# Moments of two tiles at once, and biases carried as the last row of difference weights

## The chip, the cores and the metric

The kernel runs on one core of a Trainium2 chip. The metric is device time in microseconds (us), the median of several executions. A profile is one execution, recorded instruction by instruction.

## The reference

The input u has 8 sequences of 512 steps and 128 features, in float32. Four layers follow, each added to its own input, and each fed with a layer norm without gain:

```
x = x + ssm(layernorm(x))          # diagonal state-space recurrence over time
x = x + linear(layernorm(x))       # one of 8 weight matrices (128 x 128), picked by logits, with its bias
x = x + delta_rule(layernorm(x))   # 16 heads of 8 features, a state of 8 x 8 per head, step by step
x = x + moe(layernorm(x))          # 8 experts, the best 2 of a softmax router
```

The parts that matter here:

```
def _layernorm(x, axis=-1, eps=1e-05):
    m = jnp.mean(x, axis=axis, keepdims=True)
    v = jnp.var(x, axis=axis, keepdims=True)
    return (x - m) / jnp.sqrt(v + eps)
...
def _l2_bounded(W, bound=1.0):               # in the first layer, for W_in and W_out
    sigma = jnp.linalg.svd(W, compute_uv=False)[0]
    return W / jnp.maximum(sigma / bound, 1.0)
...
out = jnp.einsum('btd,de->bte', x, W[idx]) + b[idx]          # second layer
...
logits = xf @ w_router                                        # fourth layer
h = jnp.einsum('te,ieh->tih', xf, w1) + b1                    # 8 experts, 128 -> 512
h = jax.nn.gelu(h)
out = jnp.einsum('tih,ihe->tie', h, w2) + b2
```

A row that comes out of the layer norm sums to zero over its 128 features. So for such a row, x W is the sum over the first 127 features of x_d (W_d - W_127), where W_127 is the last row of W.

## The kernel before, in words

**Tiles and groups.** A tile is 16 time steps of all 8 sequences: 128 rows of 128 features, one row on each of the 128 partitions. There are 32 tiles, taken in 8 groups of 4. Up to three layers of different groups are in work at once. The experts work on "chunks" of `GROUPS`: first one group of 4 tiles, then three times 8 tiles, then 4 tiles.

**First layers.** `input_statistics` takes the layer norm's numbers of the input of all groups early: `moments` runs bn_stats and bn_aggr for each tile on VectorE, and `factors` makes from mean and variance the factor and the shift on POOL (GpSimd). The u of later groups is loaded for that into the five buffers named `w1b`. `load_x` loads u once more for the layers themselves, into two buffers named `x`. `scanned` is the state-space layer up to its scan, `ssm_out` its output, scaled by `gain`, and `linear` the second layer, with the picked weights `wsel` and the picked bias `bsel` that POOL gathers from DRAM at the start.

**The gain.** It needs the largest singular value of W_in and of W_out. `spectral` squares W^T W `SQUARINGS` times on TensorE, for the two matrices in turn, with a trace every third step that keeps the numbers in range. The two are on VectorE and ScalarE: `copied` and `scaled` differ. At the end two sums (`total`) give the value.

**Delta rule.** `delta_in` makes keys, queries, values and beta of a group with TensorE, ScalarE and POOL, writes keys and queries to a DRAM buffer (`scratch`), and prepares small matrices (`tmat`). `delta_rule` is the recurrence. For each tile SP loads `kq` (two buffers of 2,048 columns, 1 MB each) from `scratch` and `vals` into `so`; then VectorE runs four blocks of six instructions each, one after the other, since each block needs the state that the block before leaves. There are 128 blocks. POOL and TensorE turn `so` into the tile's output x3.

**Experts.** `route` takes the layer norm of x3 into tiles `xne`, the router's logits, the two best experts and their weights. `experts` counts rows for each expert, scatters the rows by indirect DMAs on POOL's queue into a DRAM table (`places`) in which every block of 128 rows belongs to one expert, and goes through the blocks: SP loads up to four blocks of rows (`xb`) and for each block the expert's first weights (`w1b`, by a register that holds the expert's row in `w1b_dram`), TensorE makes `ph`, ScalarE the gelu into `hid`, TensorE the second product. The results go to DRAM (`results`), POOL gathers them back by row (`back`), and they are weighted and added. A chunk of 4 tiles makes 15 blocks and one of 8 makes 23: 99 in all. The weights in `w1b_dram` have 516 columns: 512 of w1, and 4 with the expert's bias, as a column for each quarter of the 512. ScalarE's gelu takes that column as its bias, one call for each quarter.

**The order.** The code does not run in the order in which it is written. Each call goes through a recorder (line 317) into a `Plan`, which knows each operation's engine, an estimated cost, and which operations it must follow. `Plan.best` makes `DRAFTS` drafts of an order by list scheduling, with due times (`nc.key`) that it changes at random from a fixed seed, and keeps the draft that ends first by its own costs. That order is then fixed: each engine and the queue of SP run their instructions one after another, and an instruction that waits holds all behind it on its engine. Almost all instructions so bear line 317 in the profile, and are told apart by the names of their buffers.

Of the kernel before, what the change touches and what calls it, by code (L numbers as in the profile page):

```python
# [17 lines left out]
P = 128  # L18
# [6 lines left out]
NHB = 4  # L25
SQUARINGS = 24
FIRST = 9
# [313 lines left out]
def _cost(engine, name, n, kw):  # L341

    if engine == "tensor":
        return 0.2 if name == "transpose" else 0.22 + 0.0019 * max(_size(kw["rhs"])[1] - 96, 0)
    if engine == "vector":
        if name == "tensor_tensor_scan":
            return 0.1 + 0.0026 * n
        return 0.19 + 0.00103 * n + (0.2 if n == 9 * 32 else 0.0)
    if engine == "scalar":
        columns = sum(isinstance(kw.get(k), bass.AP) for k in ("bias", "scale"))  # L350
        return 0.18 + 0.00085 * n + (0.0, 0.0001 * n, 0.13)[columns]
    return 0.22 + 0.0015 * n if n < 64 else 0.4 + 0.0017 * n

# [3 lines left out]
BEHIND = 8.0  # L357
DRAFTS = 60
JITTER = 15
# [7 lines left out]
def seq_kernel(  # L367
# [72 lines left out]
    def ctile(shape, name, dtype=F32):  # L440
        return const.tile(shape, dtype, tag=name, name=name)
# [18 lines left out]

    WIDE = {"both": 2 * N, "xne": P, "w1b": NHB * P + NHB, "drive": N + B, "z": N + B, "kq": NR * QN, "prod": B * BL * BL}

# [4 lines left out]
    def stile(shape, tag, dtype=F32, bufs=2):  # L467
        return turn(
            "small_" + tag, bufs, lambda name: pipe.tile(shape, dtype, tag=name, name=name)
        )[tuple(slice(0, m) for m in shape)]  # L470
# [35 lines left out]

    R_BP, R_AL, R_DB, R_G, R_B, R_QKVB, R_B1 = 0, 3, 4, 5, 6, 7, 11
    n_rows = R_B1 + NE * NHB
    rows = ptile([n_rows, P], "hid", 3)
    nc.scalar.dma_start(rows[R_BP : R_BP + 3], bp.rearrange("(c p) -> c p", p=P))  # L510
    for r, v in ((R_AL, alpha_log), (R_DB, delta_bias), (R_G, ln_g), (R_B, ln_b)):
        nc.scalar.dma_start(rows[r : r + 1], v.rearrange("(c p) -> c p", p=P))
    nc.scalar.dma_start(rows[R_QKVB : R_QKVB + 4], b_qkvb.rearrange("(c p) -> c p", p=P))
    nc.scalar.dma_start(rows[R_B1:], b1.rearrange("e (c p) -> (e c) p", p=P))
    lg_col = ctile([P, 1], "lg_col")
# [10 lines left out]
    wr = ctile([P, NE], "wr")  # L526
    nc.sync.dma_start(wr, w_router)

    b2_sb = ctile([NT * NE, NT, D], "b2_sb")
# [122 lines left out]
    def col(r):  # L652
        return cols[:, r : r + 1]


    FW = NHB * P + NHB
    w1b_dram = dram.tile([NE * P, FW], F32, tag="w1b_dram", name="w1b_dram")
    nc.key = 0.0
    nc.sync.dma_start(w1b_dram[:, 0 : NHB * P], w1.rearrange("e d f -> (e d) f"))
    nc.sync.dma_start(  # L660
        w1b_dram[:, NHB * P :].rearrange("(e p) c -> p e c", p=P),
        cols[:, R_B1:].rearrange("p (e c) -> p e c", c=NHB),
    )

# [39 lines left out]
    w_row = ctile([P, 1], "w_row", U32)  # L704
    nc.vector.tensor_copy(w_row, pk[:, 4:5])
    b_row = ctile([P, 1], "b_row", U32)
    nc.vector.tensor_copy(b_row, topi[:, 0:1])
    wsel = ctile([P, D], "wsel")
    bsel = ctile([P, D], "bsel")
    for dst, src, row in (  # L710
        (wsel, ffn_W.rearrange("e d f -> (e d) f"), w_row),
        (bsel, ffn_b, b_row),
    ):
        nc.gpsimd.indirect_dma_start(
            out=dst[:, :],
            out_offset=None,
            in_=src,
            in_offset=bass.IndirectOffsetOnAxis(ap=row[:, :1], axis=0),
        )


    def moments(src, part, bufs=2):

        n = src.shape[1]
        st = stile([P, NT, 6], "st" + part)
        mv = stile([P, NT, 2], "mv" + part, F32, bufs)[:, 0:n]
        for i in range(n):
            nc.vector.bn_stats(st[:, i, :], src[:, i, :])
            nc.vector.bn_aggr(mv[:, i, :], st[:, i, :])
        return mv  # L730

    def factors(mv, part, norms=1, bufs=2):

        n = mv.shape[1]
        rstd = stile([P, norms, NT], "rstd" + part, F32, bufs)[:, :, 0:n]
        nc.gpsimd.tensor_scalar_add(rstd[:, 0], mv[:, :, 1], LN_EPS)
        if norms == 2:

            nc.gpsimd.tensor_scalar(rstd[:, 1], mv[:, :, 1], 1.0 + LN_EPS, LN_EPS * LN_EPS, ALU.mult, ALU.add)
        nc.gpsimd.tensor_tensor(rstd, rstd, mhalf[:, 0:norms, 0:n], ALU.pow)  # L740
        shift = stile([P, norms, NT], "shift" + part, F32, bufs)[:, :, 0:n]
        nc.gpsimd.tensor_mul(shift, mv[:, :, 0].unsqueeze(1).to_broadcast([P, norms, n]), rstd)
        nc.gpsimd.tensor_scalar_mul(shift, shift, -1.0)
        return rstd, shift
# [3 lines left out]

    def normalised(src, rstd, shift, xn, norm=0):
        for i in range(src.shape[1]):  # L750
            nc.scalar.activation(
                xn[i], src[:, i, :], AF.Identity, bias=shift[:, norm, i : i + 1], scale=rstd[:, norm, i : i + 1]
            )
        return xn

    def tiles_of(v):
        return [v[:, i, :] for i in range(v.shape[1])]
# [22 lines left out]
    def over_tiles(v, n):  # L780
        return v.unsqueeze(1).to_broadcast([P, n, D])
# [93 lines left out]
    def linear(x1):  # L875

        n = x1.shape[1]
        rstd, shift = statistics(x1, "a")
        xT = ptile([P, n * P], "f", FIRST)
        nc.scalar.copy(xT, transposed(normalised(x1, rstd, shift, tiles_of(ptile([P, n, D], "f", FIRST)))))  # L880
        x1b = ptile([P, n, D], "f", FIRST)
        nc.gpsimd.tensor_add(x1b, x1, over_tiles(bsel, n))
        x2 = ptile([P, n, D], "x2", 2)
        nc.vector.tensor_add(x2, tokens_out(xT, wsel), x1b)
        return x2
# [178 lines left out]
    def route(g, x3, group):  # L1064
# [3 lines left out]
        rstd, shift = statistics(x3, "e")  # L1068
        x3n = normalised(x3, rstd, shift, [ptile([P, D], "xne", MAXT) for _ in range(NT)])
        x3T = ptile([P, N], "x3T")  # L1070
# [94 lines left out]
    def experts(group):  # L1165
# [144 lines left out]
        def hidden_of(j):  # L1310
# [16 lines left out]
            for c in range(NHB):  # L1327
# [3 lines left out]
                )  # L1331
            for c in range(NHB):
                cs = slice(c * P, (c + 1) * P)
                nc.scalar.activation(
                    hid[:, cs], ph[:, cs], AF.Gelu_apprx_tanh, bias=w1b[:, NHB * P + c : NHB * P + c + 1]
                )
            return hid
# [66 lines left out]
    sp = ctile([P, 24], "sp")  # L1404
    smax, rmax, rtr, sums, lam, sig = (sp[:, i : i + 2] for i in (0, 2, 6, 8, 12, 14))
    nc.vector.tensor_reduce(smax, w_both, AX.X, ALU.max, apply_absolute_value=True)
# [13 lines left out]
    def spectral(i, copied, scaled):  # L1420

        c = slice(i, i + 1)
        junk = ptile([P, P], ("x3T", "fin")[i])

        def power():
            return ptile([P, P], ("xbT", "xne")[i], (2, MAXT)[i])

        def total(x, y, column):

            sums_ = part[:, 2 * column + i : 2 * column + i + 1]  # L1430
            if x is y:
                nc.scalar.activation(junk, x, AF.Square, accum_out=sums_)
            else:
                nc.vector.tensor_mul(junk, x, y)
                nc.vector.tensor_reduce(sums_, junk, AX.X, ALU.add)
            at = ph_tile()[:, 0:1]
            nc.tensor.matmul(
                at, lhsT=ones, rhs=part[:, 2 * column + i : 2 * column + i + 1], start=True, stop=True
            )
            return at  # L1440

        cur, a0 = power(), ptile([P, P], f"back{i}")
        scaled(cur, w_both[:, i, :], rmax[:, c])
        factor = None
        for step in range(SQUARINGS + 1):
            bank = po_tile()
            nc.tensor.matmul(bank[:, 0:P], lhsT=cur, rhs=cur, start=True, stop=True)
            if step % 3 == 0 and step < SQUARINGS:


                trace = total(cur, cur, 0)
                nc.vector.tensor_scalar_max(rtr[:, c], trace, 1e-18)
                nc.vector.reciprocal(rtr[:, c], rtr[:, c])
                nc.vector.tensor_mul(rtr[:, c], rtr[:, c], rtr[:, c])
            cur = a0 if step == 0 else power()
            if step % 3 == 1:
                scaled(cur, bank[:, 0:P], rtr[:, c])
            else:
                copied(cur, bank[:, 0:P])
            yield  # L1460
        nc.vector.tensor_copy(sums[:, c], total(cur, a0, 0))
        nc.vector.tensor_scalar_max(rtr[:, c], total(cur, ident, 1), TINY)
        nc.vector.reciprocal(rtr[:, c], rtr[:, c])
        yield

# [3 lines left out]
    for _ in zip(  # L1469
        spectral(0, nc.vector.tensor_copy, vector_scaled), spectral(1, nc.scalar.copy, nc.scalar.mul)  # L1470
    ):
        pass
    nc.vector.tensor_mul(lam, sums, rtr)
    nc.gpsimd.tensor_tensor(sig, lam, half, ALU.pow)
# [23 lines left out]
    for g in range(1, NG):  # L1498
# [4 lines left out]
        input_statistics(g, x)  # L1503

    x2s = {g: first_layers(g) for g in range(2)}
    for g in range(NG):
# [70 lines left out]
```

## Time and profile before

| | |
|---|---|
| median of 14 runs | 772.32 us (768.63 to 777.38) |
| the profiled execution | 774.93 us, of it 773.2 us span from the first to the last instruction |
| granted TensorE clock, mean | 0.811 |
| TensorE matmul busy | 524.3 us (68%), 2,948 instructions |
| VectorE busy | 526.7 us (68%), 1,468 instructions |
| ScalarE busy | 469.1 us (61%), 1,062 instructions |
| POOL busy | 549.0 us (71%), 681 instructions |
| gelu, x396 | 114.0 us on ScalarE, 380 ns each |
| DMA | 105.94 MB, 137 GB/s in the mean |

How to read it: the busy times are means over stages with different limits, so a stage is read from the busy times in its own stretch of time. In a timeline a line gives the start, the duration, the engine, the line of the kernel, the operation, `out<-in` by the names of the buffers, the shapes, the count, and in brackets how long the engine had been idle and what ended that. `SPq` is SP's queue, which issues DMAs: the duration there is that of the issue, not of the transfer.

### The profile page before, as it was taken

The page shows a single profiled execution, that of the slowest core. Times are in us where ns is not written, and L with a number is a line of the kernel's source. Part 1 is how long each engine was busy: PE and PEld are TensorE (multiplying, and loading weights), DVE is VectorE, ACT ScalarE, POOL GpSimd, SP SyncE. Part 2 cuts the span into 40 slices and gives each one's busy share as a digit, 9 for nine tenths or more (in the row PEclk, how much of TensorE's full clock was granted, in tenths as well). Part 3 has the DMA queues.
Part 4 walks back from the last instruction along what each step waited for, and adds up shares of the span by engine and source line. Part 5 has one row for each costly group of instructions (what it writes and reads, how often), then busy time and mean ns, then how long its engine had stood idle before and what let it go on. Part 6 is the DMA issues. An engine that isn't in the chain of part 4 may idle for free. (4 is left out here: it accounts for less than half of the span.)

```text
span 773.2 us, 11166 instructions
## 1 busy us (share of the span) xinstructions
PE 524.3 (68%) x2948; PEld 408.1 (53%) x2948; DVE 526.7 (68%) x1468; ACT 469.1 (61%) x1062; POOL 549.0 (71%) x681
## 2 busy tenths in 40 slices
PE   5884664874861886894687888397893677568190
PEld 4662224453541464682465766385783576568190
DVE  5764189989997999999599999679896563000103
ACT  3855756655854899986668878248562346446060
POOL 6658575776688996998699997975887476732603
PEclk9755576786895889996698999879997699879686
DMA  3725242532435643654554864748686476656332
GB/s 105 211 73 170 64 94 60 137 76 58 115 97 150 165 119 83 178 150 136 141 136 122 206 174 123 195 127 201 184 205 170 134 189 174 162 149 183 88 97 78
DMA packets 97717, 105.94 MB, mean 137 GB/s; under 512 B 9100, under 2 KB 72535, under 8 KB 97655
## 3 DMA queue, kind: packets, MB, share of 16 engines
q1 hardware_dynamic: 92992, 96.66, 47.7%
q0 software_dynamic: 4160, 8.53, 4.0%
q8 instruction: 25, 0.41, 0.2%
q14 instruction: 38, 0.30, 0.1%
q10 hardware_dynamic: 502, 0.03, 0.0%
HBM read 81.26 MB, written 23.94 MB: 136 GB/s over the span
## 5 line engine op out<-in xcount | busy, mean ns | idle before, releaser
L317 ACT ACTIVATE hid<-ph,w1b 128x128 f32<-128x128 f32 x396 | 114.0, 380 | 79.9 <-remote 28.2
L317 PE MATMUL ph<-xbT,w1b 128*128 128x128 f32 x792 | 121.1, 297 | 29.6 <-ACT xbT L317 21.9
L317 PEld LDWEIGHTS ph<-xbT,w1b 128*128 128x128 f32 x792 | 110.2, 210 | 44.2 <-ACT xbT L317 24.3
L317 POOL DMA_INDIRECT back<-results,small_dest x64 | 63.0, 984 | 57.3 <-DVE fin L317 26.6
L317 DVE TENSOR_TENSOR so<-kq,st 128x512 f32<-128x512 f32 x128 | 87.5, 684 | 15.9 <-PE in L317 7.4
L317 DVE TENSOR_REDUCE st<-so 128x32 f32<-128x288 f32 x128 | 84.1, 657 | 3.5
L1297 PE MATMUL po<-w_sb,hid 128*128 x536 | 80.6, 288 | 8.1 <-ACT hid L317 4.9
L1297 PEld LDWEIGHTS po<-w_sb,hid 128*128 128x128 f32 x536 | 72.8, 202 | 16.2 <-issue 8.6
L1235 POOL DMA_INDIRECT places<-xne,small_dest x64 | 64.5, 1007 | 21.7 <-issue 14.1
L286 ACT ACT_TABLE_LOAD x52 | 66.7, 1283 | 6.3 <-DMA hid<-in_L_ffn_b_dram 5.4
L317 PE MATMUL po<-wo,so 128*128 128x128 f32 x256 | 44.9, 330 | 33.4 <-DVE so L317 15.3
L317 DVE TENSOR_REDUCE st<-st 128x64 f32<-128x320 f32 x128 | 63.6, 497 | 4.0
L317 PEld LDWEIGHTS po<-wo,so 128*128 128x128 f32 x256 | 41.2, 239 | 43.6 <-DVE so L317 16.5
L317 PE MATMUL in<-b,head_ones 128*128 128x512 f32 x80 | 52.1, 744 | 8.4 <-ACT kn L317 2.2
L317 DVE TENSOR_TENSOR st<-kq,st 128x256 f32<-128x256 f32 x128 | 54.7, 428 | 4.2
L317 DVE TENSOR_REDUCE st<-prod 128x32 f32<-128x128 f32 x128 | 37.6, 294 | 24.9 <-ACT upd L317 15.4
L317 PE MATMUL in<-f,wT 128*128 128x512 f32 x64 | 43.3, 769 | 15.2 <-ACT qkp L317 5.4
L1297 PE MATMUL in<-w_sb,hid 128*128 x256 | 38.0, 290 | 20.1 <-ACT hid L317 17.2
L317 POOL TENSOR_TENSOR qkp<-qkp,upd 128x512 f32<-128x512 f32 x32 | 38.9, 1216 | 17.5 <-ACT upd L317 17.5
L317 POOL TENSOR_TENSOR so<-so 128x512 f32<-128x512 f32 x24 | 30.5, 1272 | 24.7 <-DVE so L317 19.4
L317 PE MATMUL in<-b,wqkvb 128*128 128x512 f32 x64 | 41.4, 746 | 9.4 <-ACT beta L317 4.3
L317 DVE SCALAR_TENSOR_TENSOR fin<-back,small_weight,fin 128x128 f32<-128x128 f32 x16 | 5.2, 350 | 62.2 <-DMA back<-results,small_dest 57.9
(292 smaller groups left out, 1311.9 us busy)
## 6 DMA issues: line engine op xcount, KB each, us to landing
kq<-scratch SPq DMA_DIRECT2D x64, 512.0 KB
w1b<-w1b_dram SPq DMA_DIRECT2D x99, 258.0 KB
xb<-places SPq DMA_DIRECT2D x21, 256.0 KB
results<-yb SPq DMA_DIRECT2D x21, 256.0 KB
places<-yb SPq DMA_DIRECT2D x2, 1472.0 KB
x<-in_L_attn_u_dram SPq DMA_DIRECT2D x32, 64.0 KB
w1b_dram<-in_L_ffn_w_dram SPq DMA_DIRECT2D x1, 2048.0 KB
scratch<-qn SPq DMA_DIRECT2D x8, 256.0 KB
```

The costliest lines, as they stand in the source:

```text
L286: self.hw.scalar.preload_act_table_set(switch)
L317: return method(*(on(x) for x in args), **{k: on(x) for k, x in kw.items()})
L1235: rows_out = hw.gpsimd.indirect_dma_start(out=table[0 : nblk * P, :], out_offset=bass.IndirectOffsetOnAxis(ap=at, axis=0), in_=src, in_off ...
L1297: return hw.tensor.matmul(out_.on(nc.banks), lhsT=src, rhs=w2_f[:, bass.ds(at + c * P, P)], start=(c == 0), stop=(c == NHB - 1),)
```

## The change

- `moments`: one bn_stats over two tiles, read alternately, so that its two halves (count, mean and sum of squared deviations of the even and the odd elements) are the two tiles' moments. The bn_aggr is gone; `factors` divides by 128.
- Biases: the layer norm's rows keep their first 127 features, and a 1 stands in the place of the last. The weights become the difference to their last row, and the bias takes the last row's place: for `wsel`, for the router (without a bias), and for w1. So `linear` needs no addition of the bias.
- The first expert weights, once: the two halves of w1 (4 experts each) are loaded into the two `kq` buffers, the last rows of all experts, spread over all partitions, into `so` and two `xb` buffers; VectorE subtracts (`fold_weights`), and SP writes 127 partitions of each half to `w1b_dram`. Row 127 of each expert comes from b1 directly. `w1b_dram` has 512 columns.
- Gelu: one call for a block of 512 columns.
- `spectral`: 23 squarings, fewer small steps in the trace, and the closing sums made from one more product and one squaring call.
- The planner makes 150 drafts, and knows a cost for memset.

```diff
-SQUARINGS = 24
+SQUARINGS = 23
...
+    if name == "memset":
+        return 0.15 + 0.0008 * n
...
-DRAFTS = 60
+DRAFTS = 150
...
+    wr_last = ctile([P, NE], "wr_last")
+    nc.sync.dma_start(wr_last, w_router[D - 1].partition_broadcast(P))
+    nc.gpsimd.tensor_sub(wr, wr, wr_last)
...
-    FW = NHB * P + NHB
+    FW = NHB * P
     w1b_dram = dram.tile([NE * P, FW], F32, tag="w1b_dram", name="w1b_dram")
     nc.key = 0.0
-    nc.sync.dma_start(w1b_dram[:, 0 : NHB * P], w1.rearrange("e d f -> (e d) f"))
-    nc.sync.dma_start(
-        w1b_dram[:, NHB * P :].rearrange("(e p) c -> p e c", p=P),
-        cols[:, R_B1:].rearrange("p (e c) -> p e c", c=NHB),
-    )
+    nc.sync.dma_start(w1b_dram.rearrange("(e p) f -> e p f", p=P)[:, D - 1, :], b1)
+    nc.key = -100.0
+    w_parts = [ptile([P, 4, FW], "kq", 2) for _ in range(2)]
+    for h, part in enumerate(w_parts):
+        nc.sync.dma_start(part, w1[4 * h : 4 * h + 4].rearrange("e d f -> d e f"))
+    lasts = [so[:, e * FW : (e + 1) * FW] for e in range(6)] + [ptile([P, FW], "xb", 3) for _ in range(2)]
+    for e0, n, dst in ((0, 6, so[:, 0 : 6 * FW]), (6, 1, lasts[6]), (7, 1, lasts[7])):
+        row = w1[e0, D - 1]
+        nc.sync.dma_start(
+            dst.rearrange("p (e f) -> p e f", f=FW), bass.AP(row.tensor, row.offset, [[0, P], [D * FW, n], [1, FW]])
+        )
+
+    def fold_weights():
+        for h, part in enumerate(w_parts):
+            nc.key = -75.0
+            for i in range(4):
+                nc.vector.tensor_sub(part[:, i], part[:, i], lasts[4 * h + i])
+            to = w1b_dram[4 * h * P : 4 * (h + 1) * P].rearrange("(e p) f -> p e f", p=P)
+            nc.sync.dma_start(to[0 : P - 1], part[0 : P - 1])
...
         (wsel, ffn_W.rearrange("e d f -> (e d) f"), w_row),
+        (wlast, ffn_W.rearrange("e d f -> (e d) f"), last_row),
         (bsel, ffn_b, b_row),
...
+    nc.vector.tensor_sub(wsel, wsel, wlast)
+    nc.vector.scalar_tensor_tensor(wsel, bsel, ident[:, P - 1 : P], wsel, ALU.mult, ALU.add)
...
-        for i in range(n):
-            nc.vector.bn_stats(st[:, i, :], src[:, i, :])
-            nc.vector.bn_aggr(mv[:, i, :], st[:, i, :])
+        for i in range(0, n, 2):
+            nc.vector.bn_stats(
+                mv[:, i : i + 2].rearrange("p i s -> p (i s)"), src[:, i : i + 2, :].rearrange("p i d -> p d i")
+            )
...
-        nc.scalar.copy(xT, transposed(normalised(x1, rstd, shift, tiles_of(ptile([P, n, D], "f", FIRST)))))
-        x1b = ptile([P, n, D], "f", FIRST)
-        nc.gpsimd.tensor_add(x1b, x1, over_tiles(bsel, n))
+        xn = ptile([P, n, D], "f", FIRST)
+        nc.gpsimd.memset(xn[:, :, D - 1 : D], 1.0)
+        nc.scalar.copy(xT, transposed(normalised(x1, rstd, shift, tiles_of(xn), 0, D - 1)))
         x2 = ptile([P, n, D], "x2", 2)
-        nc.vector.tensor_add(x2, tokens_out(xT, wsel), x1b)
+        nc.vector.tensor_add(x2, tokens_out(xT, wsel), x1)
...
-            for c in range(NHB):
-                cs = slice(c * P, (c + 1) * P)
-                nc.scalar.activation(
-                    hid[:, cs], ph[:, cs], AF.Gelu_apprx_tanh, bias=w1b[:, NHB * P + c : NHB * P + c + 1]
-                )
+            nc.scalar.activation(hid, ph, AF.Gelu_apprx_tanh)
...
-            if step % 3 == 0 and step < SQUARINGS:
-                trace = total(cur, cur, 0)
-                nc.vector.tensor_scalar_max(rtr[:, c], trace, 1e-18)
+            if step % 3 == 0:
+                nc.vector.tensor_scalar_max(rtr[:, c], squares(cur), 1e-18)
                 nc.vector.reciprocal(rtr[:, c], rtr[:, c])
-                nc.vector.tensor_mul(rtr[:, c], rtr[:, c], rtr[:, c])
...
-        nc.vector.tensor_copy(sums[:, c], total(cur, a0, 0))
-        nc.vector.tensor_scalar_max(rtr[:, c], total(cur, ident, 1), TINY)
+        bank = po_tile()[:, 0:P]
+        nc.tensor.matmul(bank, lhsT=a0, rhs=cur, start=True, stop=True)
+        nc.vector.tensor_scalar_max(rtr[:, c], squares(cur), TINY)
         nc.vector.reciprocal(rtr[:, c], rtr[:, c])
+        nc.vector.tensor_mul(a0, cur, bank)
+        nc.vector.tensor_reduce(part[:, 2 + i : 3 + i], a0, AX.X, ALU.add)
+        nc.vector.tensor_mul(lam[:, c], rtr[:, c], summed(1))
...
+    for x in [ptile([P, D], "xne", MAXT) for _ in range(MAXT)]:
+        nc.gpsimd.memset(x[:, D - 1 : D], 1.0)
...
+    fold_weights()
     x2s = {g: first_layers(g) for g in range(2)}
```

## The prediction

> **What bounds the kernel now.** I read the page first (VectorE's busy tenths in 40 slices), then the busy times by stage.
>
> ```profile
> span 773.2 us, 11166 instructions
> DVE  5764189989997999999599999679896563000103
> ```
>
> ```profile
> 0.00:99.00 99.00, 67.62 (x215) 43.57 (x216) 48.79 (x220) 61.25 (x142) 63.15 (x98) 0.69 0.45 127
> 99.00:640.00 541.00, 380.08 (x2144) 291.97 (x2144) 462.95 (x1187) 355.90 (x758) 428.75 (x525) 0.84 0.54 140
> 640.00:773.20 133.20, 76.65 (x593) 72.61 (x591) 14.96 (x62) 52.00 (x163) 57.06 (x60) 0.80 0.49 131
> ```
>
> After the span the columns are PE, PEld, DVE, ACT, POOL, then clock, DMA share and GB/s. There are three stages with three limits. Up to about 99 us no engine is full: a chain of short steps. From 99 to 640 the VectorE is busy 463 of 541 us: the recurrence, 128 blocks of six instructions. After 640 the VectorE is nearly done and TensorE, ScalarE and gathers alternate. So an edit is worth something in the first stage only if it moves the recurrence's start, and in the second only if it shortens VectorE. The timelines of VectorE, ScalarE and the SP queue show what sets that start.
>
> ```profile
> 70.22 0.69 DVE L317 TENSOR_TENSOR x<-in,f 128x512 f32<-128x512 f32 x1 [5.81 <-ACT f L317]
> ...
> 92.60 0.69 DVE L317 TENSOR_TENSOR drive<-f,in 128x512 f32<-128x512 f32 x1 [19.97 <-POOL f L317]
> ...
> 104.96 0.67 DVE L317 TENSOR_TENSOR so<-kq,st 128x512 f32<-128x512 f32 x1
> ```
>
> ```profile
> 82.60 1.64 ACT L317 ACTIVATE f<-x,small_shifti,small_rstdi 128x128 f32<-128x128 f32 x4
> ...
> 88.68 0.67 ACT L317 ACTIVATE qn<-in,nbq 128x512 f32<-128x512 f32 x1
> ```
>
> ```profile
> 28.12 10.05 SPq L317 DMA_DIRECT2D w_sb<-in_L_ffn_w_dram  x2
> ...
> 59.81 2.71 SPq L317 DMA_DIRECT2D x<-in_L_attn_u_dram  x4
> 64.40 3.83 SPq L317 DMA_DIRECT2D places<-yb  x2
> 89.37 0.36 SPq L317 DMA_DIRECT2D scratch<-qn  x1
> 90.28 0.36 SPq L317 DMA_DIRECT2D scratch<-kn  x1
> 92.00 2.51 SPq L317 DMA_DIRECT2D kq<-scratch  x4
> ```
>
> The first product with kq, at 104.96, is the recurrence's start. It needs the scratch writes and kq loads of SP's queue, and these need ScalarE, which at 82.60 reads the x loaded from 59.81 (third group). SP issues in order: a transfer stuck there holds all that follows.
>
> **The change part by part.** The sum goes against the profiled execution: 773.2 span, 774.9 with what lies around it, 2.6 above the median of 772.3, so 2.6 is taken off at the end.
>
> *Moments.* A tile now costs a bn_stats and a bn_aggr: in the VectorE timeline the four of one group begin at 59.78, 60.21 and 60.60, 0.395 us apart, 0.79 a pair. After: one bn_stats over 256 elements. From 128 to 256 I add 0.13 (products grow from 428 ns at 256 columns to 684 at 512, 1.0 ns a column) to 0.27: 0.40, with a gap 0.43. It reads in steps of 512 B; the one row with such steps, so's reduction (288 elements, 657 ns; the contiguous one of 320 takes 497), is 1.47 times dearer per element, so 0.60 at worst. A pair saves 0.19 to 0.36; behind the start lie 44 pairs (14 of "a", 14 of "b", 16 of "e"): 8 to 16 us of VectorE, 12 taken. The VectorE is busy 86% there, so 10 off the end. The 20 other pairs lie ahead of the start, beside idle VectorE: 0.
>
> *Gelu.* 396 calls of 380 ns start 0.25 us apart, 1.14 us a block; one call over 512 columns from PSUM with tanh's bias takes 688 (row f<-in,cols). That is 99 x 0.45 = 45 us of ScalarE. But the chain that ended last holds 0.3% of "ACT hid", 2.3 us, and waits of TensorE on it lie mostly in stalls that end elsewhere: 3 off, between 0 and 8. The first product of the second layer now waits 0.69 instead of 0.37; the next block's first layer covers it, else 0.3 a block on the few uncovered.
>
> *Bias in linear.* Eight additions on POOL of 1,266 ns go, eight memsets of four columns come (a memset of 8 columns: 0.11): 9 us of POOL, not what VectorE waits for: 0.
>
> *Squaring.* 25 steps run from 9.4 to 51.8 us, 1.7 each; one goes, and the end (51.8 to gain at 58.5) loses about 1.5. So gain comes 3 us earlier, worth 3 if nothing else is late.
>
> *Router and linear weights.* A row load, one more POOL gather (about 1 us, before 30) and small subtractions; wsel is read at 68: 0.
>
> *Expert weights.* Now w1 goes DRAM to DRAM in one transfer (26.18), with a 16 KB bias write; nothing waits for it before the experts. After: w1 to both kq buffers (2 x 1 MB), last rows to 128 partitions (2 MB), eight subtractions of 512 columns (684 each, 5.5 us on a VectorE with 20 us of idle: 0), and two writes from SBUF of 127 partitions x 4 x 2,048 B. A kq load must wait until its buffer has been written out, and the writes stand in SP's queue ahead of x, scratch and kq. Their duration decides.
>
> How many DMA engines does such a write use? In the trace's semaphore records a transfer's end is one count from each engine it ran on. The load of one row (alpha_log) ends with 1 count, of three rows (bp) with 3, of four (b_qkvb) with 4, x (outer count 8) with 8, wqkvb (128 partitions) with 16. All are the largest divisor of the outer count up to 16. 127 has only 1. The Trainium skill, "DMA: Bandwidth & Descriptors", section "Why a DMA increments its semaphore by 16 and not by 1", states that divisor rule and names 127 partitions as a case of one engine; no run here shows 127 yet.
>
> What does one engine take? From the DMA view of 24 to 46 us:
>
> ```profile
> q1 hardware_dynamic: 4612, 4.83, 74.1%
> ```
>
> 74.1% of 16 engines for 22 us is 261 us of engine time for 4.83 MB: 54 us per MB. A write has 508 packets, 1.04 MB: 56 us on one engine, 3.5 on sixteen. The trace's packets of 2,048 B took 89 ns in the median (45 us), the lower end, since one engine alone contends less. I take 48, so 96 for both.
>
> When do they start? The 2 MB of w1 now moves at 26; the loads are 4 MB, at the 226 GB/s of that stretch 18 us: in SBUF at about 44, subtracted by 45 (30 at the earliest, 60 at the latest, as w2's issue blocks SP for 10). Both writes end at 45 + 96 = 141 (30 + 90 = 120; 60 + 112 = 172). What is late next: if only scratch and kq stand behind them, the recurrence starts some 8 us later (issue of kq to its landing, and the scratch write), 149, +44. If ScalarE stands before x of the third group as now, 82.60 becomes 143, +60, and all behind it moves along. I take +50. The 3 us of the squarings are hidden by it: 0. VectorE idles 78 us between 99 and 640, so a late start gives some back: 5 (0 to 10).
>
> *Order.* Costs and 150 drafts instead of 60 give another written order; stalls like ScalarE's wait of 17.2 us before "hid" near 717 can move: 0, plus or minus 10.
>
> Sum: +50 - 5 - 10 - 3 = +32: 774.9 + 32 = 806.9 profiled, about 804 in the median.
>
> **The rivals.** *A, not slower: the writes spread.* If 127 partitions go on 16 engines, each write is 3.5 us, done by about 55, before kq is wanted at 92. The point from which it decides is three engines or more: 2 x 56 / 3 = 37 us, done by 82. Then gain's 3, moments' 10 and gelu's 3 remain: 772.3 - 16 = 756. For it: nothing in the trace with an odd large count; against: every count I could read follows divisors.
>
> *B, one engine but mostly hidden.* If w1 is loaded ahead of everything, the writes start near 25 and end at 115; kq then lands near 120, +15, and 5 + 10 + 3 pay for it: about 770. For it: SP has some 45 us of issues that could be put in any order; against: the x loads come first by their dates.
>
> *C, worse.* Writes at 56 us each from 60: end 172, start +85: about 840.
>
> **How the numbers follow.** The forecast has 0.68, A 0.17, B 0.10, C 0.05. The forecast's own range: a start 25 later with savings of 22 gives 775, one 70 later with savings of 8 gives 834. To hold 8 in 10 with A's lower side, B and C it is 754 to 846. This measurement can tell about 0.3% from no change, 2.3 us. Faster: A, half of B: 0.22; same: 0.04; slower: 0.74.
>
> **What would show it.** Right: two SP writes into w1b_dram near 45 us, a DMA share near 0.06 (one of 16) for most of 50 to 140, the first "so<-kq" near 150, from there VectorE about 10 us shorter; bn_stats x64 at 0.40 to 0.60 us; gelu x99 near 0.69. Wrong: the writes landing within 5 us (A), or kq's first product before 115 (B), or gelu's time coming off the end one for one.

## The result, and the profile after

The changed kernel takes 823.83 us (median of 10 runs, 822.72 to 826.24), the kernel before 772.63 (47 runs): a ratio of 1.0665, 95% interval 1.0642 to 1.0687. It is 51.2 us slower. The profiled execution has a span of 821.9 us at a granted clock of 0.793.

The page of the changed kernel, three of its rows: VectorE's and the DMA's busy tenths in 40 slices of 20.5 us.

```profile
span 821.9 us, 10612 instructions
DVE  5662000299998999799979999977999453000102
DMA  5690001334343673633465566447787266267432
```

VectorE has three empty slices, from 82 to 144 us, with one at two tenths before and after them. In the same slices the DMA engines are at 0 and 1 tenths: neither computing nor, by the mean of 16 engines, much moving. Busy time by stage of the changed kernel (columns as before):

```profile
0.00:99.00 99.00, 47.45 (x193) 35.38 (x193) 41.88 (x154) 44.40 (x109) 54.87 (x99) 0.67 0.47 138
99.00:150.00 51.00, 2.80 (x8) 1.44 (x8) 0.75 (x2) 6.97 (x16) 2.59 (x3) 0.50 0.07 27
150.00:690.00 540.00, 390.96 (x2160) 297.98 (x2160) 448.17 (x1071) 331.83 (x580) 424.50 (x531) 0.85 0.54 143
690.00:821.90 131.90, 76.90 (x587) 74.12 (x587) 13.55 (x49) 31.60 (x56) 57.92 (x59) 0.77 0.47 132
```

A stage of 51 us is new. In it VectorE works for 0.75 us, and the DMA share is 0.07 at 27 GB/s: one engine of 16 is 0.0625. The clock granted there is 0.50. SP's queue, ScalarE and VectorE of the changed kernel show what is waited for:

```profile
40.88 7.09 SPq L317 DMA_DIRECT2D w_sb<-in_L_ffn_w_dram  x2
48.07 5.96 SPq L317 DMA_DIRECT2D w1b<-in_L_attn_u_dram  x4
54.08 0.46 SPq L317 DMA_DIRECT2D places<-yb  x1
54.64 39.02 SPq L317 DMA_DIRECT2D w1b_dram<-kq  x2
93.80 44.31 SPq L317 DMA_DIRECT2D x<-in_L_attn_u_dram  x4
```

```profile
142.92 1.71 ACT L317 ACTIVATE f<-x,small_shifti,small_rstdi 128x128 f32<-128x128 f32 x4 [69.84 <-DMA x<-in_L_attn_u_dram]
```

```profile
57.08 0.98 DVE L317 TENSOR_TENSOR kq<-kq,xb 128x512 f32<-128x512 f32 x1
...
148.71 0.69 DVE L317 TENSOR_TENSOR drive<-f,in 128x512 f32<-128x512 f32 x1 [75.81 <-POOL f L317]
...
172.78 0.68 DVE L317 TENSOR_TENSOR so<-kq,st 128x512 f32<-128x512 f32 x1
173.50 0.67 DVE L317 TENSOR_REDUCE st<-so 128x32 f32<-128x288 f32 x1
```

The last subtraction ends at 58.06. The two writes are issued from 54.64, and SP stands at their issue for 39 us and at that of x behind them for 44. Two writes are 1,016 packets of 2,048 bytes. In the trace they follow one another without a gap from 60.85 to 142.14: a packet takes 84 ns, and the next starts 80 ns after it, which makes 81.3 us. In the trace's semaphore records each write ends with the count of a single engine, at 101.83 and at 142.49. The first begins when the queue's transfers ahead of it are through: from 55.00 to 61.15 the engines move 3,426 packets of 512 bytes, most of them the 1,472 KB of `places`, issued at 54.08.

Of the first load of x, seven of its eight engines are through by 136.11 and the eighth at 142.90. At 142.92 ScalarE gets the x that it has waited for, 69.84 us idle, and the recurrence starts at 172.78 instead of 104.96. From there to the end it is 649.1 us, where it was 668.2. So the start lost 67.8 us, and what lies behind it gained 19.1. These two depend on the mark. In the kernel before, VectorE does 4.0 us of other work between the first product and the next instruction of the recurrence:

```profile
109.64 0.65 DVE L317 TENSOR_REDUCE st<-so 128x32 f32<-128x288 f32 x1
```

In the changed kernel that instruction follows at once, at 173.50. Counted from it, the start lost 63.9 us and the rest gained 15.2.

### The profile page after: what moved, and what is told of

The parts are those of the page before. It is cut to its first block, busy times and chain, and to the rows that moved or that the text cites. A ratio compares the mean times of both kernels' runs of the same rounds, so it can differ in the third digit from the quotient of the medians.

```text
span 821.9 us, 10612 instructions
## 1 busy us (share of the span) xinstructions
PE 518.1 (63%) x2948; PEld 408.9 (50%) x2948; DVE 504.3 (61%) x1273; ACT 414.8 (50%) x759; POOL 539.9 (66%) x691
## 5 line engine op out<-in xcount | busy, mean ns | idle before, releaser
L317 ACT ACTIVATE hid<-ph 128x512 f32<-128x512 f32 x99 | 58.1, 597 | 148.6 <-remote 72.5
L317 PE MATMUL ph<-xbT,w1b 128*128 128x128 f32 x792 | 115.9, 292 | 12.0 <-ACT xbT L317 8.0
L1330 PE MATMUL po<-w_sb,hid 128*128 x552 | 86.2, 300 | 53.0 <-ACT hid L317 46.2
L317 POOL DMA_INDIRECT back<-results,small_dest x64 | 62.3, 974 | 46.7 <-DVE fin L317 25.5
L317 POOL TENSOR_TENSOR f<-f,f 128x512 f32<-128x512 f32 x24 | 30.3, 1270 | 69.9 <-ACT f L317 69.9
L317 PE MATMUL po<-wo,so 128*128 128x128 f32 x304 | 54.6, 336 | 30.8 <-DVE so L317 12.1
L317 PEld LDWEIGHTS po<-wo,so 128*128 128x128 f32 x304 | 50.0, 246 | 42.5 <-DVE so L317 14.9
L317 PE MATMUL in<-ident,f 128*128 128x128 f32 x64 | 15.8, 356 | 84.8 <-ACT f L317 79.0
L317 PEld LDWEIGHTS in<-ident,f 128*128 128x128 f32 x64 | 9.8, 174 | 92.7 <-ACT f L317 84.0
L317 DVE TENSOR_TENSOR drive<-f,in 128x512 f32<-128x512 f32 x8 | 5.4, 680 | 75.8 <-POOL f L317 75.8
L317 ACT ACTIVATE f<-x,small_shifti,small_rstdi 128x128 f32<-128x128 f32 x32 | 13.6, 487 | 70.1 <-DMA x<-in_L_attn_u_dram 69.8
```

What stands on the lines that cost most here:

```text
L317: return method(*(on(x) for x in args), **{k: on(x) for k, x in kw.items()})
L1330: return hw.tensor.matmul(out_.on(nc.banks), lhsT=src, rhs=w2_f[:, bass.ds(at + c * P, P)], start=(c == 0), stop=(c == NHB - 1),)
```

## The experiments

Every kernel below except those with another seed runs exactly the order that the planner wrote for the changed kernel: the planner is shown the same operations and costs, and only what an operation issues is replaced. With 60 drafts instead of 150 the planner writes that same order too. So the 150 drafts of the change are without any effect. In the code shown, `hw` issues to the engine directly, past the recorder `nc`. The runs were made in three sets on different chips. Each set has its own runs of the kernel before, and differences in us are taken within a set, but for those against the changed kernel, whose runs stand beside a kernel before of 772.63 us.

### The writes in rows that divide

```diff
-            nc.sync.dma_start(to[0 : P - 1], part[0 : P - 1])
...
+                hw.sync.dma_start(to[0:112], part[0:112])
+                return hw.sync.dma_start(to[112 : P - 1], part[112 : P - 1])
```

> The changed kernel with each write of 127 partitions cut into one of 112 and one of 15, in the same written order of everything. Theory (a write runs on as many engines as the largest divisor of its outer count up to 16): 16 and 15 engines, each half out in under 10 us, both halves by about 65 instead of 138; the first so<-kq falls from 172.8 to about 103 (100 to 110), and the time to about 756 (750 to 764), under the kernel before. Rival 1 (the kq buffers, the subtractions or the new order hold the start): start above 150, time above 800. Rival 2 (all writes of less than 128 partitions are slow, or writes from SBUF to DRAM are): 815 to 825, as the changed kernel.

Measured: 757.25 us (753.06 to 761.56), ratio to the kernel before (773.51 here) 0.9785, interval 0.9749 to 0.9821. SP's queue of this kernel, and VectorE's first `so<-kq`:

```profile
54.63 4.49 SPq L687 DMA_DIRECT2D w1b_dram<-kq  x1
59.16 0.91 SPq L688 DMA_DIRECT2D w1b_dram<-kq  x1
60.16 1.74 SPq L687 DMA_DIRECT2D w1b_dram<-kq  x1
61.96 1.66 SPq L688 DMA_DIRECT2D w1b_dram<-kq  x1
63.74 4.21 SPq L317 DMA_DIRECT2D x<-in_L_attn_u_dram  x4
```

```profile
106.69 0.68 DVE L317 TENSOR_TENSOR so<-kq,st 128x512 f32<-128x512 f32 x1
```

The same bytes leave the same buffers from the same moment, in four transfers instead of two, and x is issued 30 us earlier and at once. In the semaphore records the writes of 112 rows end with 16 counts each and those of 15 rows with 15, and all 1,016 packets move between 60.37 and 68.30. Against the changed kernel the time falls by 66.6 us and the start by 66.1 (the time by 67.5 if each kernel is taken against its own runs of the kernel before; it is known to some 3 us). So the stall is worth its length, and no catching up is seen. Both rivals of this run fall: it is not the order, the subtractions or the buffers as such, and a write of fewer than 128 partitions is not slow in itself.

The second kernel differs in one row.

```diff
-            nc.sync.dma_start(to[0 : P - 1], part[0 : P - 1])
...
+                hw.sync.dma_start(to[0:113], part[0:113])
+                return hw.sync.dma_start(to[113 : P - 1], part[113 : P - 1])
```

> The same cut one row further, 113 and 14: as many transfers and the same order, but 113 is prime. Divisor theory: one engine carries 113/127 of the bytes, so each large write takes 113/127 of its 42 us, 38; the writes end near 129 instead of 138, the first so<-kq comes near 163, and the time is about 814 (808 to 820). Rival (what helped in the cut was two transfers instead of one, or smaller ones): as the kernel with 112 and 15, about 756.

Measured: 812.94 us (809.12 to 815.76), ratio 1.0521 (1.0494 to 1.0548), start at 165.29. Expected were 814 and 163. SP's queue of this kernel, and its first `so<-kq`:

```profile
55.16 4.38 SPq L687 DMA_DIRECT2D w1b_dram<-kq  x1
59.59 30.49 SPq L688 DMA_DIRECT2D w1b_dram<-kq  x1
90.18 0.46 SPq L687 DMA_DIRECT2D w1b_dram<-kq  x1
90.69 35.20 SPq L688 DMA_DIRECT2D w1b_dram<-kq  x1
```

```profile
165.29 0.68 DVE L317 TENSOR_TENSOR so<-kq,st 128x512 f32<-128x512 f32 x1
```

One row more in the large write and one less in the small one is 55.7 us. The number of transfers and their mean size are those of the run before, so the rival falls. The semaphore records show the engines: each write of 113 rows ends with one count (98.01 and 134.51), each of 14 rows with 14, of which 13 come early (by 92.38 for the first) and the last just behind the large write (98.34). The packets run from 61.51 to 134.49, 73.0 us. At 80 ns that is 912 packets: the 904 of the large writes, and the 8 that a fourteenth of the small ones has, so they share that engine. In SP's list the small write is the line with the long duration: SP stands at the issue of the transfer behind the slow one. (The end at 138 that the expectations name for the changed kernel is that of SP's issue of x, 93.80 + 44.31; its last packet ended at 142.14.)

### Gelu

```diff
-            nc.scalar.activation(hid, ph, AF.Gelu_apprx_tanh)
...
+                for c in range(NHB):
+                    cs = slice(c * P, (c + 1) * P)
+                    hw.scalar.activation(hid[:, cs], ph[:, cs], AF.Gelu_apprx_tanh)
```

> 112 and 15 rows, and the gelu of a block in four calls of 128 columns again (without the bias column), in the same written order. It takes 99 x (4 x about 0.28 less 0.60), some 45 to 55 us, more of ScalarE. Theory of the prediction (ScalarE is off the path but for single blocks): 3 us slower than 112 and 15 alone (0 to 8). Rival (ScalarE sets the tail and the order's stalls): 15 us or more.

Measured: 756.18 us (755.40 to 758.50), ratio 0.9778 (0.9752 to 0.9804), against 757.25 with one call: no difference. The groups of the kernel with one call (112 and 15 rows), and of that with four:

```profile
L317 ACT ACTIVATE hid<-ph 128x512 f32<-128x512 f32 x99 | 58.0, 597 | 140.5 <-remote 65.1 <-PE ph L317 56.2 <-PE po L1335 11.5
```

```profile
L1374 ACT ACTIVATE hid<-ph 128x128 f32<-128x128 f32 x396 | 77.2, 289 | 134.7 <-remote 70.3 <-PE ph L317 51.5 <-issue 8.3
```

The group's busy time grows by 19.2 us, less than the 45 expected, since calls without a bias column take 289 ns and overlap, and its idle time falls by 5.8. ScalarE idles 140 us ahead of these calls in any case; what is saved in the call is waited in front of the next. The calls of the kernel before took 380 ns with their bias column and 114.0 us together, so this run gives back only 19.2 of the 56.0 us that the change takes off ScalarE here. What the other 36.8 are worth, no run shows.

### Moments

```diff
-            nc.vector.bn_stats(
-                mv[:, i : i + 2].rearrange("p i s -> p (i s)"), src[:, i : i + 2, :].rearrange("p i d -> p d i")
-            )
...
+                for k in (i, i + 1):
+                    hw.vector.bn_stats(st[:, k, :], src[:, k, :])
+                    hw.vector.bn_aggr(mv[:, k, 1:3], st[:, k, :])
```

> 112 and 15 rows, and the moments tile by tile again (bn_stats and bn_aggr, the factor 1/128 taken out of the numbers behind), in the same written order. A pair of tiles costs 1.58 instead of 0.43 at the most and 0.79 instead of 0.43 at the least by the starts read before; behind the recurrence's start lie 44 pairs. Theory (VectorE bounds the middle, 86% of its time is worth time): 44 x 0.36 x 0.86 = 14 us slower than 112 and 15 alone (8 to 20). Rival (VectorE's idle time takes it): under 4 us.

Measured: 770.03 us (765.58 to 772.23), ratio 0.9956 (0.9936 to 0.9976): 12.8 us more than with 112 and 15 rows alone. Two groups of this kernel, and then the one that stands in their place in the changed kernel:

```profile
L765 DVE BATCH_NORM_STATS2 small_ste<-x 128x6 f32<-128x128 f32 x32 | 8.7, 272 | 0.0
...
L766 DVE BATCH_NORM_AGGREGATE small_mve<-small_ste 128x2 f32<-128x6 f32 x32 | 5.8, 183 | 1.1
```

```profile
L317 DVE BATCH_NORM_STATS2 small_mve<-x 128x6 f32<-128x256 f32 x16 | 6.8, 427 | 0.2
```

The read of two tiles in turn, in steps of 512 bytes, costs 427 ns for 256 elements: 155 ns more than 128 in a row. No run has 256 elements in a row beside it, so what the steps cost is not measured; an estimate from the products of the kernel before (428 ns at 256 columns, 684 at 512, so 1.0 ns a column) gives 128 ns for 128 more, which leaves some 27 for the steps. For the "e" tiles 14.5 us of VectorE become 6.8. VectorE's busy time falls from 528.3 to 505.1 us, and 12.8 of these 23.2 come off the time; 2.8 of them stand ahead of the recurrence's start (109.46 against 106.69).

### The order, and another queue

The second set, on a chip where the kernel before takes 729.57 us:

```diff
-        dice, kept = random.Random(1), None
+        dice, kept = random.Random(2), None
```

> 112 and 15 rows, with another seed for the planner's drafts, so another written order of the same work. The prediction gave the order plus or minus 10 us: between 747 and 767. Rival (orders that the planner holds for equally good are equally good on the chip): within 2 us of 757.

Measured: 713.62 us (712.85 to 716.50), ratio 0.9793 (0.9750 to 0.9836). That ratio is the same as in the first set with the first seed, but ratios do not carry over between these chips (below), so this run alone does not settle the order. The start moved to 101.90, and the rest of the span was 610.3 us.

```diff
-            nc.sync.dma_start(to[0 : P - 1], part[0 : P - 1])
...
+                return tc.keep_in_program_order(hw.gpsimd.dma_start(to[0 : P - 1], part[0 : P - 1]))
```

> The changed kernel with its writes of 127 partitions whole, issued at the same place of the written order from POOL's queue instead of SP's. Theory (one engine whatever the queue, and the kq buffers must wait; only what merely stood behind the writes in SP's queue is let go): the writes end near 138 as now, x of the third group lands near 65, the first so<-kq comes some 10 us after the writes, near 149, and the time is near 799 (790 to 806), between the two kernels: the part of the 66 us that is the queue's is the rest. Rival 1 (the divisor rule is one of SP's queue; POOL's spreads the rows): start near 106, time near 757. Rival 2 (it is the buffers alone): 820.

Measured: 735.00 us (733.52 to 737.14), ratio 1.0086 (1.0061 to 1.0110), start at 138.90. Neither the theory nor a rival is right as it was put. POOL's writes, with the DMA issues' row (the last number is the time to landing), SP's `places` and x, and ScalarE of this kernel:

```profile
48.49 4.66 POOL L687 DMA_DIRECT2D w1b_dram<-kq  x1 [0.65 <-DVE xbT L317]
...
63.73 4.60 POOL L687 DMA_DIRECT2D w1b_dram<-kq  x1
```

```profile
w1b_dram<-kq POOLq DMA_DIRECT2D x2, 1016.0 KB, 50.9
```

```profile
55.09 2.47 SPq L317 DMA_DIRECT2D places<-yb  x1
72.57 27.22 SPq L317 DMA_DIRECT2D x<-in_L_attn_u_dram  x4
```

```profile
107.64 0.49 ACT L317 ACTIVATE f<-x,small_shifti,small_rstdi 128x128 f32<-128x128 f32 x1 [25.55 <-DMA x<-in_L_attn_u_dram]
```

The 50.9 us to landing are known of the second write alone, which so lands at 114.6; the last count of the first one's semaphore comes at 108.70, 60.2 us after its issue. So neither is spread over 16 engines. The 508 packets of the two, of 4,096 bytes here, move from 55.91 to 113.78, up to 12 in a us. At 159 ns each, one engine could move 6 in a us, so the two writes run side by side on two engines, which SP's two did not. The Trainium skill, "DMA: Bandwidth & Descriptors", section "Why a DMA increments its semaphore by 16 and not by 1", states that a transfer that fits few engines takes the lowest-numbered ones from queues such as SP's, and from POOL's the next ones of a cursor that goes round. Both traces agree with that, 81.3 us in a row against 57.9 together, though no record names the engine. They end at 113.8, where the theory, one engine for both, had 138. What it got wrong most is x: on another queue than the writes it was still held at its issue, until 99.8, and ScalarE waited 25.55 us for it. The semaphore records tell where it was held. Of `places`, just ahead of x in SP's queue, 15 of 16 engines are through by 68.33, and the last at 104.47. Of the first load of x, six of eight are through by 91.79, the other two at 97.11 and 107.62. So transfers of SP's queue have a share on the engines of POOL's writes, and land only when that share has come through: from 70 to 90 us SP's queue moves 4.9 packets of 512 bytes in a us, where it moved 259 from 55 to 66. Another queue takes x out of the line behind the writes, but not off their engines. How long SP itself stands at such an issue, no run explains.

### Two small things that were put down as nothing

Each of these two was seen in the profile of the kernel with 112 and 15 rows. Its POOL and its ScalarE:

```profile
41.00 0.20 POOL L317 TENSOR_TENSOR wr<-wr,wr_last 128x8 f32<-128x8 f32 x1 [5.63 <-DMA wr_last<-in_L_ffn_w_router_dram]
41.84 1.22 POOL L317 DMA_INDIRECT wsel<-in_L_ffn_W_dram,w_row  x1 [0.64 <-DVE sp L317]
```

```profile
45.70 0.72 ACT L317 ACTIVATE f<-f,minus_one 128x512 f32<-128x512 f32 x1 [4.83 <-POOL f L317]
46.32 0.25 ACT L317 COPY xne<-in 128x128 f32<-128x128 f32 x1
```

The router's last row is loaded behind 32 loads of u on SP's queue. POOL waits 5.63 us for it to subtract eight columns that nobody needs before the router. Behind that stand two gathers and a product, behind the product ScalarE, and behind ScalarE a copy of the squarings. In the change below, `lambda: None` keeps the subtraction's place in the plan and issues nothing there.

```diff
-    nc.gpsimd.tensor_sub(wr, wr, wr_last)
+    nc.add("gpsimd", lambda: None, [wr_last, wr], [wr], _cost("gpsimd", "", NE, {}))
...
-    nc.gpsimd.tensor_mul(gain, gain, lg_col)
...
+        tc.keep_in_program_order(hw.gpsimd.tensor_mul(gain, gain, lg_col))
+        return hw.gpsimd.tensor_sub(wr, wr, wr_last)
```

> 112 and 15 rows, and POOL's subtraction of the router's last row, at 41.00 in the profile after 5.63 us of waiting for its load, put behind gain's last product; the rest in the same written order. Theory (this wait held the gathers, a product of POOL, the ScalarE instruction that needs it and the squaring's copy behind that one, 4.2 us on TensorE): gain's reciprocal comes at about 57 instead of 61.3, the first so<-kq at about 103 instead of 106.7, the time 753 (750 to 755). Rival (the writes in SP's queue, done at 63.6, set the start by now): start unmoved, 757.

Measured: 696.84 us (694.73 to 699.37) on the second chip, ratio 0.9562 (0.9520 to 0.9604). Gain's reciprocal came at 58.03 and the start at 103.30, 3.3 and 3.4 us earlier than on the first chip without it, but the time against the kernel before fell by far more than that. And the other small thing, POOL's additions:

```diff
-        nc.gpsimd.tensor_scalar_mul(shift, shift, -1.0)
...
+            tc.keep_in_program_order(hw.gpsimd.tensor_scalar_mul(shift, shift, -1.0))
+            tc.keep_in_program_order(hw.gpsimd.tensor_add(spare, x1[:, 0:2], x1[:, 0:2]))
+            return hw.gpsimd.tensor_add(spare, x1[:, 2:4], x1[:, 2:4])
```

> 112 and 15 rows, and POOL does the work of the removed additions again, two of 256 columns a group behind the shift's factor, with an output that nobody reads; same written order. About 11 us more of POOL. Prediction (not what VectorE waits for): 0, within 2 us of 757. Rival (POOL's 70% hides stalls of VectorE): 4 to 11 us slower.

Measured: 707.93 us (707.30 to 709.64), ratio 0.9711 (0.9670 to 0.9752). Taken against the 0.9785 of the first chip the added work made it faster, while its start came later, at 110.51. So the first chip's ratio is no base for this one, and the base was run again with both, in a third set, where the kernel before takes 775.21 us.

> The kernel with 112 and 15 rows again, beside the next three, since the second set of runs fell on another chip, where the kernel before takes 729.6 us instead of 773.5. If the ratio to the kernel before carries over from chip to chip it is 0.9785 again (0.975 to 0.982), and the additions of POOL made the kernel faster, which nothing explains. If less of the time of this kernel follows the granted clock, or more, it is another one: under 0.971 on the faster chip would make the additions cost something.

> 112 and 15 rows and the router's subtraction later, again, beside its base. Theory: the start moves by 3.4 us (it did) and the rest follows, so 3.4 us less than 112 and 15 rows alone (0.995 of it). Rival (a stall further on that the shift resolves): over 8 us less, as the two sets of runs, each against its own kernel before, say (0.9562 against 0.9785).

> The same with the work of the removed additions on POOL again (output that nobody reads). Prediction's 0 for POOL: within 2 us of the one before it. Theory from the profile (POOL is full from 57 to 85 us, and the start moved from 106.7 to 110.5 with the additions): 4 to 11 us more.

| kernel (112 and 15 rows) | us | ratio, interval | start of recurrence |
|---|---|---|---|
| again as it was | 755.78 (754.29 to 758.54) | 0.9775, 0.9729 to 0.9822 | 105.92 |
| router's subtraction later | 750.14 (749.25 to 755.26) | 0.9723, 0.9674 to 0.9771 | 102.94 |
| the same, and POOL's additions | 759.54 (757.74 to 762.22) | 0.9821, 0.9774 to 0.9868 | 106.52 |

The base repeats on this third chip (0.9775 for the first one's 0.9785). The router's wait is worth 5.6 us, 3.0 of them at the start. The six runs of the two kernels touch at their edges, so this cannot be told from the 3.4 of the theory; the rival of over 8 was the second chip's. The additions cost 9.4 us, 3.6 at the start and the rest behind it. Their groups:

```profile
L786 POOL TENSOR_TENSOR spare<-x 128x256 f32<-128x256 f32 x8 | 5.3, 668 | 0.6
L785 POOL TENSOR_TENSOR spare<-x 128x256 f32<-128x256 f32 x8 | 4.9, 607 | 0.0
```

That is 10.2 us of POOL for 9.4 us of time, nearly one for one, on an engine that is 72% busy in the mean. It stands right behind the factor of the layer norm that ScalarE waits for. In the kernel before the same work stood elsewhere, where its planner had put it, so 9.4 us is what it costs in this order, and only stands in for what its removal gained.

> 112 and 15 rows and the router later, with the planner's seed 5, whose order the planner itself holds for 10.6 us shorter (694.1 against 704.7 by its own costs; seed 2, run before, 705.8). If its costs describe the chip: some 8 to 12 us less than the first seed. Rival (orders differ by stalls that the planner's costs do not know): anything within 15 us either way.

Measured: 755.88 us (753.17 to 756.46), ratio 0.9766 (0.9720 to 0.9812), against 750.14 with the first seed: 5.7 us more, where the planner's own costs said 10.6 less. The planner's end did not rank these two orders, which it held 10.6 us apart.

The kernel with rows that divide and the router's subtraction later is the best seen: 750.14 us, 2.8% under the kernel before and 9% under the changed one (0.9723 against 1.0665).

## Why the prediction was right, and where it was not

Forecast were 804 us and slower, by one mechanism; it came out at 824 by that mechanism, inside the range. Rival A (writes spread), B (mostly hidden) and C (a start 85 later) did not happen.

| term | forecast, us | measured, us | by |
|---|---|---|---|
| writes on one engine, with the catch-up | +50 - 5 | +66.6 | 112 and 15 rows |
| moments | -10 | -12.8 | moments by one |
| gelu | -3 | +1.1 (none) | gelu by four, a third of the saving |
| linear's additions on POOL | 0 | -9.4, in this order | both |
| router's and linear's rows | 0 | +5.6 (router's wait) | router again |
| sum | +32 | +51.1 | against +51.2 |

The squaring less, the order and the rest of gelu are what is left of the sum: 0.1 us. The terms come from different sets and each is known to some 3 us, so that they meet this closely is chance.

*How many engines.* Right. The divisor rule was argued from transfers of 1, 3, 4, 8 and 128, and 127 behaves as it says. The semaphore records count the engines: 1 for 127 and 113 rows, 16 for 112, 15 for 15, 14 for 14. The runs with 113 against 112 rows, one apart, show what it costs, and 112 and 15 that the cure is in the shape.

*Their duration.* 48 us each was taken; it was 40.6, 508 packets 80 ns apart. The median packet read from the trace of before, 89 ns, was the better basis, and still too long. In the changed kernel's trace such a packet took 116 ns in the median at 52 to 55 us, where the DMA engines are nearly full (a share of 0.92 from 40 to 55), and 84 when one engine moved alone. The 54 us per MB came from a stretch with all engines contending, and I leaned a little towards it.

*Their start.* 45 was taken; they began at 60.9. The data were there as forecast: the first subtraction ran at 26.91, the fourth, the last of the first half, ended at 43.6. But SP's queue issued the first write only at 54.64, behind the load of w2 (7 us of issue from 40.88) and four loads of u (5.96 from 48.07), and then the 1,472 KB of `places` kept the engines for another 6.2. The prediction had named w2's issue as the reason for a latest start of 60, and did not put it into the value it took; `places` it did not count. The start is 15.9 us late and the two writes 14.7 shorter, and that the two errors cancel is luck: both writes end at 142.1, forecast 141.

*What is late next.* This is the step that failed in size. I gave two paths, +44 if only scratch and kq stand behind, +60 if ScalarE stands before x of the third group, and took +50 between them. They are exclusive, and the second one happened: the forecast "82.60 becomes 143" is 142.92 in the trace. That it came so close owes to the lucky end of the writes. From there to the start it was 29.9 us instead of 22.4. Of these 7.5 us, 4.0 are VectorE's work (the last of the delta rule's `b` and `tmat`, a group's scaling and moments) that stood behind the first product before and stands ahead of it in the new order; for the other 3.5 no cause is shown. 60.3 and 7.5 are the 67.8.

*Catch-up.* 5 (0 to 10) was taken, from VectorE's idle time in the middle. Starts 66.1 us apart gave times 66.6 apart: 0, to some 3 us.

*Moments.* Right: behind the start they are worth 10.0, as forecast. The forecast's 0.40 was the lower bound of the instruction and 0.422 to 0.427 is what it takes. The 20 pairs ahead of the start, put at 0, are worth 2.8.

*Gelu.* The forecast's lower end. 597 ns instead of 688; for the part of the saving that was tested, the place off the path was right.

*POOL's additions.* Wrong, 0 against 9.4. I looked whether VectorE waits for POOL in the middle stage. My reading, which no run isolates, is that what matters is what stands behind the addition on POOL: the small products for the next factors. In the stretch from 57 to 85 us of the kernel with the router's subtraction later (on the second chip), in which the start is made, POOL is busy for 25.5 of the 28 us.

*Squaring and router.* The forecast had gain 3 us earlier. It came 2.7 later: 61.21 for 58.52. With the router's subtraction later (the third set) it came at 57.59, so 0.9 of the 3 us are there. I had called the router's row "a row load and small subtractions: 0" and looked at when its result is needed (late), not at what its wait holds on POOL (the gathers and all behind them). The same rule was written for the transfers and not applied to this one.

## What to carry to other kernels

Before a transfer is shaped, look at its outermost count: a count with a small largest divisor runs on few engines, and one row more or less decides over tens of microseconds; cut 127 as 112 and 15. A transfer that keeps one engine busy delays every later one that has a share there, from another queue too. Of every added instruction, however small, ask what it waits for and what is queued behind it on its engine; the time at which its result is used says nothing about that. When two paths are possible after a delay, do not take the mean of them: find in the written order which one is first.

## What was not expected of the hardware

- A transfer on one engine holds the issuing queue: SP stood 39.0 and 44.3 us at the issue of transfers, one of them x with 64 KB a tile. A DMA that is 0.07 busy was the bound of the stage from 99 to 150 us.
- A transfer lands with its slowest engine: with POOL's writes on two engines, `places` had 15 of its 16 counts at 68.33 and the last at 104.47.
- One engine alone moved packets of 2,048 bytes out of SBUF every 80 ns, 26 GB/s, without gaps.
- bn_stats over 256 elements, alternating between two tiles, takes 424 ns where 128 in a row take 270.
- The chip of the second set runs the same kernel before in 729.57 us instead of 773.51, at higher granted clocks (0.844 to 0.855 for the four kernels there, 0.823 to 0.835 for their like on the others), and ratios between kernels differ there by up to 1.7%: router's subtraction later is 0.9562 there and 0.9723 elsewhere.
